# Storing the 0/1 matrices of layer 0 and loading them in layer 2, with two vector additions moved

## The chip, the cores and the metric

The kernel runs on 1 core of one Trainium2 chip, as one program. The metric is the device time of one execution, in microseconds (us). The engines are TensorE (PE in the profile, with its weight loads as PEld), VectorE (DVE), ScalarE (ACT), GpSimd (POOL) and SyncE (SP). They run side by side, each through its own instructions in order, and wait for one another through semaphores. The 16 DMA engines of the core are shared by the transfers that SP, ACT and POOL issue.

## The reference

The network has 50,000 nodes with 64 features and 25,000 edges, sorted by target node, and four residual layers. Cut to what matters:

```python
h = relu(layernorm(x));  x = x + L0(h)   # message passing: relu([h[src],h[dst]] @ W + b), mean by target, update
h = relu(layernorm(x));  x = x + L1(h)   # graph convolution: weighted sum by target, then @ W.T + b
h = relu(layernorm(x));  x = x + L2(h)   # attention over the edges of a target, Wo, FiLM, layer norm,
                                         # gelu MLP, then layer norm with ln2_g and ln2_b
h = relu(layernorm(x));  x = x + L3(h)   # exp(-t L) h as a Taylor series: powers of a sparse matrix B on h
```

Each layer gathers node rows for the edges and sums edge rows into nodes. Layers 0, 1 and 2 sum by target node, layer 3 by source node.

## The kernel before

The nodes are cut into NQ = 49 groups of 1,024 (8 blocks of 128). The edges of a group fill 5 tiles of 128 slots (TL = 245 tiles in all). A tile can only hold edges of a few blocks (the tables `BT` and `TB`), and for these pairs of tile and block the kernel makes 0/1 matrices on DVE by comparing numbers.

- `node_hot` (L1881) makes `s.noh`, nodes x slots: 8 comparisons a group, against the row of keys that `load_keys` (L1876) reads for all partitions. TensorE uses it to bring rows of node tables to the edges' slots (`to_slots`, and the loop of `logits` in layer 2).
- `slot_hot` (L1889) makes `s.soh`, slots x nodes: 5 comparisons a group. TensorE uses it to sum edges into nodes (`to_sums`, `to_nodes`).

Layers 0 and 2 make both matrices from the same keys; layer 1 makes `soh` alone; layer 3 has another order of edges and its own `soh`.

Each layer is a software pipeline over the 49 groups. `pipeline` (or `Steps` in layer 2) runs one stage of each group in flight, oldest group first, and a new group enters at each step. Layer 0 has the stages fetch, hots, message, sums, update, project; layer 1 has fetch, scaled, sums, turn, product. Layer 2 has an "up" pipeline (fetch, hots, logits) and a "down" pipeline (fetch2, message, sums, attend, turn, close, product, finish) with a `softmax` between them for each of 4 batches of 12 or 13 groups: while batch k goes up, batch k-1 goes down. So the first batch goes up alone and the last goes down alone. Layer 3 (fetch, scaled, sums) computes B h; then come the second power by pairs and the higher powers on short lists.

Rows of other nodes come by indirect DMA that POOL issues, 5 a group and layer (`gather`, L1006: `ga`, `gt`, `kvg`, `y`). POOL also issues the transfers of the lists for the higher powers (`nmap`, `lgot`, `lrow`). `build_lists` is cut into small pieces, and `lists_pace` lets some of them into the program after each stage (0.5 a stage in layer 0, 0.4 in layer 1, 1.2 in layer 2). A list of one level is found from the list of the level before, through DRAM: POOL scatters, SP loads (`lback`), DVE compares, POOL scatters and gathers again.

The order of each engine's instructions is laid down when the program is built, by a scheduler that starts from the order of the source and from its own estimate of times. Every instruction after that waits in its engine's line. Tiles live in pools with `bufs` buffers: a tile's next writer waits until the last reader is done. In layers 0 and 2 the pools have 2 buffers unless a tile says otherwise; the DMAs that SP and ACT issue take 8 semaphores in turn.

Other lines that matter: layer 1's `sums` adds (L2074) `x2` and stores it in `x2tab` from ACT (L2075); layer 2's `close` loads it again (L2357), and `finish` multiplies by ln2_g (L2378), adds ln2_b to x2 (L2379), adds both (L2380), takes the norm and relu to `h`, stores `h` in `h3tab` (L2383), adds `h` (L2384) and stores the sum in `xstab` (L2385). Layer 3's `sums` loads that sum and adds the first term of the series (L2502).

Of the kernel before, what the change touches and what calls it, by code (L numbers as in the profile page):

```python
# [59 lines left out]
GRP = ((0, 1), (1, 2), (3, 1), (4, 2), (6, 2))  # L60
OHW = (0, 384, 768, 1152, 1664, 1920)

POLY = np.ones(1)
# [903 lines left out]
def fast(ctx: ExitStack, tc: tile.TileContext, a: dict, out: bass.AP, flag: bass.AP):  # L967
# [913 lines left out]
    def node_hot(pool, s):  # L1881

        s.noh = pool.tile([P, 8, 2 * P], BF16, name="noh")
        for j in range(8):
            t0, n = BT[j]
            nc.vector.tensor_scalar(s.noh[:, j, :n * P], s.keys[:, t0 * P:(t0 + n) * P], pblk[:, j:j + 1], None,  # L1886
                                    op0=OP.is_equal)
# [10 lines left out]
    def to_slots(po, s, tab, start=True):  # L1898

        for i in range(5):  # L1900
            b0, nb = TB[i]
            for j in range(b0, b0 + nb):
                c = (i - BT[j][0]) * P
                for k in range(3):
                    nc.tensor.matmul(po[:, i, :], s.noh[:, j, c:c + P], tab[:, j, k * D:k * D + D],
                                     start=(start and j == b0 and k == 0), stop=(j == b0 + nb - 1 and k == 2))
# [68 lines left out]
    with tc.tile_pool(name="l0c", bufs=1) as cp, tc.tile_pool(name="l0", bufs=2) as pool, \  # L1975
# [67 lines left out]


    with tc.tile_pool(name="l1c", bufs=1) as cp, tc.tile_pool(name="l1", bufs=2) as pool, \
            tc.tile_pool(name="pl1", bufs=1, space=PSUM) as ps:
        b1l = bias_rows(cp, row_bcast("L1_gnn_b", pool=cp), "b1l")
        wkv = cp.tile([P, 4 * D], F32, name="wkv")
        cen = ident_less_mean(cp)
# [19 lines left out]
        def sums(q, s):  # L2069
# [34 lines left out]
    with tc.tile_pool(name="l2c", bufs=1) as cp, tc.tile_pool(name="l2", bufs=2) as pool, \  # L2104
# [105 lines left out]
        nc.vector.tensor_copy(zb[:, 1:2], pb)  # L2210
        g2n, b2n = row_bcast("L2_gnn_ln2_g", pool=cp), row_bcast("L2_gnn_ln2_b", pool=cp)

# [6 lines left out]
        def fetch(q, s):  # L2219
# [4 lines left out]
            nc.sync.dma_start(s.qt.rearrange("p b k d -> p b (k d)"), nodes(qtab, q))  # L2224
            load_keys(pool, q, s)
            s.typ = pool.tile([NE3, RW], F16, name="typ", bufs=2)
            nc.sync.dma_start(s.typ, ttab[q:q + 1, :].to_broadcast([NE3, RW]))

        def hots(q, s):
            s.types = pool.tile([NE3, RW], BF16, name="types")  # L2230
            nc.vector.tensor_scalar(s.types, s.typ, typei, None, op0=OP.is_equal)
            node_hot(pool, s)

        def logits(q, s):
# [18 lines left out]
            for i in range(5):  # L2253
                nc.tensor.matmul(pe[:, i, :], s.types[:, i * P:(i + 1) * P], etab[:, KW:], start=True, stop=False)
                b0, nb = TB[i]
                for j in range(b0, b0 + nb):
                    c = (i - BT[j][0]) * P
                    for k in range(3):
                        nc.tensor.matmul(pe[:, i, :], s.noh[:, j, c:c + P], s.qt[:, j, k, :], start=False,
                                         stop=(j == b0 + nb - 1 and k == 2))  # L2260
# [107 lines left out]
        def finish(q, s):  # L2368
# [9 lines left out]
            nc.vector.tensor_mul(x3, x3, along(g2n, 8))  # L2378
            nc.vector.tensor_add(s.x2, s.x2, along(b2n, 8))  # L2379
# [4 lines left out]
            nc.vector.tensor_add(x3, x3, h)  # L2384
            nc.scalar.dma_start(nodes(xstab, q), x3)  # L2385
# [95 lines left out]
    with tc.tile_pool(name="mps", bufs=1, space=PSUM) as mps, tc.tile_pool(name="l3", bufs=2) as pool, tc.tile_pool(name="pl3", bufs=2, space=PSUM) as ps:  # L2481
        def fetch(q, s):
# [177 lines left out]
```

## Time and profile before

| | us |
|---|---|
| median of 9 runs | 3656.36 (3638.07 to 3663.84) |
| the profiled execution, its own time | 3658.54 |
| its span | 3656.4 |
| lists and tables before layer 0 | 0 to about 650 |
| layer 0 | about 650 to 1390 |
| layer 1 | about 1390 to 1815 |
| layer 2 | about 1815 to 2860 |
| layer 3, B h | about 2860 to 3205 |
| second power, higher powers | about 3205 to 3656 |

The borders come from the starts of the lines that belong to each layer; neighbouring layers overlap a little. The profiled execution's time is 2.1 us over its span and 2.2 us over the median. In the views, "busy" is the union of an engine's instructions, "x" their number, and the time after the bar is how long the engine sat idle before them and what ended that.

### The profile page before, as it was taken

The page shows a single profiled execution, that of the slowest core. Times are in us where ns is not written, and L with a number is a line of the kernel's source. Part 1 is how long each engine was busy: PE and PEld are TensorE (multiplying, and loading weights), DVE is VectorE, ACT ScalarE, POOL GpSimd, SP SyncE. Part 2 cuts the span into 40 slices and gives each one's busy share as a digit, 9 for nine tenths or more (in the row PEclk, how much of TensorE's full clock was granted, in tenths as well). Part 3 has the DMA queues.
Part 4 walks back from the last instruction along what each step waited for, and adds up shares of the span by engine and source line. Part 5 has one row for each costly group of instructions (what it writes and reads, how often), then busy time and mean ns, then how long its engine had stood idle before and what let it go on. Part 6 is the DMA issues. An engine that isn't in the chain of part 4 may idle for free. (4 is left out here: it accounts for less than half of the span.)

```text
span 3656.4 us, 63671 instructions
## 1 busy us (share of the span) xinstructions
PE 2533.4 (69%) x21828; PEld 1787.6 (49%) x21828; DVE 2662.8 (73%) x8365; ACT 1325.7 (36%) x3056; POOL 2090.3 (57%) x1997
## 2 busy tenths in 40 slices
PE   7897774699999746777579766677677464466620
PEld 3324664577777634566455433344333354355520
DVE  9999998777778637999878766788888665455310
ACT  0002552222223314777504443445478333332000
POOL 0477777733333766666376775765100577775786
PEclk9755555755556766888758776778789675566555
DMA  1003772744445415877665333333222345488221
GB/s 53 6 4 111 210 231 85 199 123 114 118 120 144 125 32 156 239 234 237 182 197 150 103 102 96 99 114 108 67 91 77 113 126 153 148 232 229 44 25 11
DMA packets 528804, 457.79 MB, mean 125 GB/s; under 512 B 282147, under 2 KB 388802, under 8 KB 528340
## 3 DMA queue, kind: packets, MB, share of 16 engines
q1 hardware_dynamic: 361204, 263.52, 25.2%
q10 hardware_dynamic: 94032, 139.60, 11.0%
q0 software_dynamic: 73232, 50.49, 7.4%
q8 instruction: 174, 2.85, 0.3%
q14 instruction: 162, 1.33, 0.1%
HBM read 217.09 MB, written 237.38 MB: 124 GB/s over the span
## 5 line engine op out<-in xcount | busy, mean ns | idle before, releaser
L1006 POOL DMA_INDIRECT y<-h3tab,sptr x245 | 257.2, 1050 | 326.2 <-DVE soh L1894 251.8
L1006 POOL DMA_INDIRECT ga<-atab,nrs x245 | 246.8, 1007 | 327.2 <-DVE z L2003 157.8
L1006 POOL DMA_INDIRECT kvg<-kvtab,nrs x245 | 249.6, 1019 | 177.0 <-issue 64.6
L1006 POOL DMA_INDIRECT gt<-g1tab,nrs x245 | 253.1, 1033 | 149.9 <-issue 65.1
L1934 PEld LDWEIGHTS <-soh 128*128 128x128 bf16 x4410 | 224.2, 118 | 207.2 <-issue 193.5
L1924 PE MATMUL pa<-soh,m 128*64 128x256 bf16 (+1 forms) x2646 | 287.1, 334 | 38.0 <-ACT m L2006 27.3
L1006 POOL DMA_INDIRECT raw<-otab,nrd x196 | 195.0, 995 | 191.9 <-DVE bad L1152 132.5
L1011 POOL DMA_INDIRECT stab<-raw,pf x196 | 206.9, 1056 | 59.7 <-issue 59.7
L1924 PEld LDWEIGHTS <-m 128*64 128x64 bf16 x2646 | 179.6, 141 | 123.4 <-issue 52.8
L1006 POOL DMA_INDIRECT lgot<-nmap,ldst x183 | 184.6, 1009 | 60.8 <-issue 52.7
L1934 PE MATMUL po<-y,soh 128*128 128x64 bf16 x2205 | 123.9, 231 | 135.7 <-DVE y L1086 73.3
L1131 DVE TENSOR_REDUCE ln_v<-ln_sq 128x8 f32<-128x512 f32 x294 | 196.4, 679 | 24.9 <-ACT ln_sq L1144 18.9
L1894 DVE TENSOR_SCALAR soh<-it,key 128x384 bf16<-128x384 f16 (+2 forms) x735 | 206.2, 323 | 4.6 <-PE pa L1924 4.4
L1006 POOL DMA_INDIRECT y<-ftab,ldst x140 | 140.0, 1000 | 84.2 <-issue 74.0
L1144 ACT ACTIVATE ln_sq<-ln_xc 128x512 f32<-128x512 f32 x196 | 121.0, 626 | 175.5 <-DVE ln_xc L1142 164.1
L1886 DVE TENSOR_SCALAR noh<-keys,pblk 128x256 bf16<-128x256 f16 (+1 forms) x784 | 178.8, 290 | 3.9 <-DMA keys<-ktab 3.9
L1086 DVE TENSOR_TENSOR y<-y 128x320 f32<-128x320 f32 (+1 forms) x196 | 75.6, 390 | 144.1 <-ACT y L2493 120.7
L1189 PE MATMUL pab<-wab,tr 64*128 64x128 f32 x784 | 148.1, 431 | 32.6 <-ACT tr L1176 32.6
L1934 PE MATMUL po<-g,soh 128*128 128x64 bf16 x2205 | 121.0, 214 | 66.3 <-DVE g L1086 66.0
L1132 ACT ACTIVATE ln_v<-ln_v,epsc 128x8 f32<-128x8 f32 x294 | 83.4, 296 | 227.5 <-DVE ln_v L1131 205.4
L2352 PE MATMUL ph<-tr,w1z 128*128 128x512 f32 x196 | 144.4, 827 | 27.2 <-ACT tr L2346 27.0
L1189 PEld LDWEIGHTS pab<-wab,tr 64*128 64x128 f32 x784 | 134.1, 319 | 51.6 <-ACT tr L1176 51.3
(571 smaller groups left out, 7488.5 us busy)
## 6 DMA issues: line engine op xcount, KB each, us to landing
kvtab<-kv SPq DMA_DIRECT2D x49, 512.0 KB
xs<-xstab SPq DMA_DIRECT2D x98, 256.0 KB
ftab<-f ACTq DMA_DIRECT2D x98, 256.0 KB
xt<-in_x SPq DMA_DIRECT2D x96, 256.0 KB
btab<-bt ACTq DMA_DIRECT2D x49, 384.0 KB
bt<-btab SPq DMA_DIRECT2D x49, 384.0 KB
qtab<-qt ACTq DMA_DIRECT2D x49, 384.0 KB
qt<-qtab SPq DMA_DIRECT2D x49, 384.0 KB
```

Of the source, the lines that this page charges most:

```text
L1006: return nc.gpsimd.indirect_dma_start(out=dst, out_offset=None, in_=tab[:, :], in_offset=IndirectOffsetOnAxis(ap=idx, axis=0))
L1011: return nc.gpsimd.indirect_dma_start(out=tab[:, :], out_offset=IndirectOffsetOnAxis(ap=idx, axis=0), in_=src, in_offset=None, bounds_chec ...
L1086: nc.vector.tensor_sub(x3[:, :, k, :], x3[:, :, k - 1, :], h[:, :, k - 1, :])
L1131: nc.vector.tensor_reduce(v, sq, AX.X, OP.add)
L1132: nc.scalar.activation(v, v, AF.Sqrt, bias=epsc, scale=1.0 / D)
L1144: nc.scalar.activation(sq, xc, AF.Square)
L1189: nc.tensor.matmul(pab[:, i, :], s.tr[r, i, :], wab[r, :], start=True, stop=True)
L1886: nc.vector.tensor_scalar(s.noh[:, j, :n * P], s.keys[:, t0 * P:(t0 + n) * P], pblk[:, j:j + 1], None, op0=OP.is_equal)
L1894: nc.vector.tensor_scalar(oh[:, OHW[i]:OHW[i + 1]], it16[:, b0 * P:(b0 + n) * P], keys[:, q, i:i + 1], None, op0=OP.is_equal)
L1924: nc.tensor.matmul(o, l, r, start=first, stop=last)
L1934: nc.tensor.matmul(po[:, j, :], oh[:, c:c + P], msg[:, i, k, :], start=(not started and i == t0 and k == 0), stop=(end and (not started or ...
L2352: nc.tensor.matmul(ph, w1z[h], s.tr, start=True, stop=True)
```

## The change

Layer 0 stores both matrices of each group in a new DRAM table, `noh` from SP and `soh` from ACT (491,520 bytes each). Layer 2 no longer makes them: it loads `noh` in the stage fetch of the up pipeline, in place of the keys, and `soh` in fetch2 of the down pipeline, each with 3 buffers. `noh` is stored without gaps (`NOH`), 1,920 columns. Layer 1 adds ln2_b to x2 before it stores it, in a tile of its own, so that layer 2 need not. Layer 2 stores its x without `h`; layer 3 loads `h` beside it and adds it in its stage scaled.

```diff
+NOH = (0, 128, 384, 640, 896, 1152, 1408, 1664)
+    ohtab = dram.tile([NQ * P, 2, OHW[-1]], BF16, name="ohtab")
...
     def node_hot(pool, s):
-        s.noh = pool.tile([P, 8, 2 * P], BF16, name="noh")
+        s.noh = pool.tile([P, OHW[-1]], BF16, name="noh")
...
         def message(q, s):                       # layer 0
+            nc.sync.dma_start(ohtab[P * q:P * q + P, 0, :], s.noh)
+            nc.scalar.dma_start(ohtab[P * q:P * q + P, 1, :], s.soh)
             pe = ps.tile([P, 5, D], F32, name="pe", bufs=2)
...
             nc.vector.tensor_add(x2, s.x1, po)   # layer 1, sums
-            nc.scalar.dma_start(nodes(x2tab, q), x2)
+            x2b = pool.tile([P, 8, D], F32, name="x2b")
+            nc.vector.tensor_add(x2b, x2, along(b2n, 8))
+            nc.scalar.dma_start(nodes(x2tab, q), x2b)
...
-            load_keys(pool, q, s)                # layer 2, fetch
+            s.noh = pool.tile([P, OHW[-1]], BF16, name="noh", bufs=3)
+            nc.sync.dma_start(s.noh, ohtab[P * q:P * q + P, 0, :])
...
-            node_hot(pool, s)                    # layer 2, hots
...
+            s.soh = pool.tile([P, OHW[-1]], BF16, name="soh", bufs=3)   # layer 2, fetch2
+            nc.sync.dma_start(s.soh, ohtab[P * q:P * q + P, 1, :])
...
-            s.soh = slot_hot(pool, key, q)       # layer 2, message
...
-            nc.vector.tensor_add(s.x2, s.x2, along(b2n, 8))   # layer 2, finish
             nc.vector.tensor_add(x3, x3, s.x2)
...
             nc.scalar.dma_start(nodes(h3tab, q), h)
-            nc.vector.tensor_add(x3, x3, h)
             nc.scalar.dma_start(nodes(xstab, q), x3)
...
+            s.h = pool.tile([P, 8, D], F32, name="h", bufs=3)   # layer 3, fetch
+            nc.sync.dma_start(s.h, nodes(h3tab, q))
...
             s.soh = slot_hot(pool, skey.rearrange("p (q i) -> p q i", i=5), q)   # layer 3, scaled
+            nc.vector.tensor_add(s.xs, s.xs, s.h)
```

More of the change, by code (lines that the diff above doesn't have):

```diff
@@ L1881, in node_hot @@
     def node_hot(pool, s):
-        s.noh = pool.tile([P, 8, 2 * P], BF16, name="noh")
+        s.noh = pool.tile([P, OHW[-1]], BF16, name="noh")
         for j in range(8):
             t0, n = BT[j]
-            nc.vector.tensor_scalar(s.noh[:, j, :n * P], s.keys[:, t0 * P:(t0 + n) * P], pblk[:, j:j + 1], None,
+            nc.vector.tensor_scalar(s.noh[:, NOH[j]:NOH[j] + n * P], s.keys[:, t0 * P:(t0 + n) * P], pblk[:, j:j + 1], None,
                                     op0=OP.is_equal)
@@ L1902, in to_slots @@
             for j in range(b0, b0 + nb):
-                c = (i - BT[j][0]) * P
+                c = NOH[j] + (i - BT[j][0]) * P
                 for k in range(3):
-                    nc.tensor.matmul(po[:, i, :], s.noh[:, j, c:c + P], tab[:, j, k * D:k * D + D],
+                    nc.tensor.matmul(po[:, i, :], s.noh[:, c:c + P], tab[:, j, k * D:k * D + D],
                                      start=(start and j == b0 and k == 0), stop=(j == b0 + nb - 1 and k == 2))
@@ L2047, in fast @@
         b1l = bias_rows(cp, row_bcast("L1_gnn_b", pool=cp), "b1l")
+        b2n = row_bcast("L2_gnn_ln2_b", pool=cp)
         wkv = cp.tile([P, 4 * D], F32, name="wkv")
@@ L2210, in fast @@
         nc.vector.tensor_copy(zb[:, 1:2], pb)
[L2211 removed]
+        g2n = row_bcast("L2_gnn_ln2_g", pool=cp)
         batches = [(0, 13), (13, 12), (25, 12), (37, 12)]
@@ L2256, in logits @@
                 for j in range(b0, b0 + nb):
-                    c = (i - BT[j][0]) * P
+                    c = NOH[j] + (i - BT[j][0]) * P
                     for k in range(3):
-                        nc.tensor.matmul(pe[:, i, :], s.noh[:, j, c:c + P], s.qt[:, j, k, :], start=False,
+                        nc.tensor.matmul(pe[:, i, :], s.noh[:, c:c + P], s.qt[:, j, k, :], start=False,
                                          stop=(j == b0 + nb - 1 and k == 2))
```

## The prediction

> **What bounds the kernel now.** I read first the busy time of each engine by stage, because the whole-span shares (DVE 73%, PE 69%) average over stages with different limits. The columns are the stretch, its length, busy us of PE, PEld, DVE, ACT and POOL with the number of instructions, the granted TensorE clock, the share of the DMA engines and GB/s.
>
> ```profile
> core 0: us, PE busy (x) PEld busy (x) DVE busy (x) ACT busy (x) POOL busy (x), PEclk, DMA share, GB/s
> 650.00:735.00 85.00, 60.58 (x802) 49.08 (x802) 65.36 (x236) 26.73 (x71) 62.41 (x64) 0.82 0.89 227
> 735.00:1170.00 435.00, 420.71 (x3696) 336.38 (x3692) 335.04 (x1220) 113.42 (x291) 147.45 (x144) 0.57 0.44 120
> 1170.00:1390.00 220.00, 138.03 (x1414) 110.79 (x1413) 124.34 (x409) 51.72 (x130) 138.47 (x145) 0.69 0.31 88
> 1420.00:1780.00 360.00, 275.41 (x3239) 218.65 (x3237) 331.12 (x943) 265.61 (x814) 226.81 (x220) 0.85 0.78 234
> 1815.00:1910.00 95.00, 66.53 (x745) 49.82 (x745) 69.10 (x293) 8.62 (x35) 69.86 (x72) 0.50 0.69 201
> 1910.00:2070.00 160.00, 134.03 (x1197) 81.18 (x1197) 132.80 (x396) 76.66 (x134) 115.66 (x112) 0.82 0.44 131
> 2070.00:2360.00 290.00, 186.49 (x1314) 110.49 (x1313) 201.20 (x641) 115.48 (x196) 205.20 (x197) 0.71 0.32 95
> 2360.00:2610.00 250.00, 188.76 (x1398) 110.33 (x1397) 212.09 (x730) 122.92 (x208) 123.72 (x114) 0.78 0.34 106
> 2610.00:2860.00 250.00, 168.83 (x822) 84.88 (x820) 206.48 (x430) 171.15 (x251) 0.00 (x0) 0.81 0.23 79
> 2890.00:3200.00 310.00, 163.71 (x2245) 143.16 (x2246) 177.12 (x447) 108.68 (x309) 235.25 (x224) 0.63 0.47 142
> ```
>
> The limits differ. Layer 0 (rows 1 to 3): DMA near its limit for the first 85 us (0.89), then PE (421 of 435 us), then POOL. Layer 1 (row 4): DVE, 331 of 360 us. Layer 2 is rows 5 to 9, cut at the softmaxes; I call them A to E. B h (row 10): POOL. POOL's waits show an "issue" of 0.3 us before nearly every indirect DMA, so POOL is full at busy + 0.31 x count: A 92 of 95 us, B 150 of 160, C 266 of 290, D 159 of 250, E 0, and B h 305 of 310. So in A to C, POOL's gathers and lists set the pace whatever DVE does; only D and E can be DVE's.
>
> Then what POOL waited for in D (us in total, times, longest):
>
> ```profile
> POOL nmap L1011 <- DVE lval L1639: 28.7, 2, 20.7
> POOL lrow L1011 <- DVE ldest L1545: 25.4, 2, 19.6
> POOL kvg L1006 <- DVE lnrow L1635: 18.1, 1, 18.1
> POOL nmap L1011 <- DVE vv L2249: 13.2, 1, 13.2
> POOL lrow L1011 <- DVE vv L2249: 6.1, 1, 6.1
> ```
>
> All 91 us of them end with DVE: here the lists wait in DVE's line. Last, the groups that the change touches (busy us, mean ns, idle before):
>
> ```profile
> L1894 DVE TENSOR_SCALAR soh<-it,key 128x384 bf16<-128x384 f16 (+2 forms) x735 | 206.2, 323 | 4.6 <-PE pa L1924 4.4
> L1886 DVE TENSOR_SCALAR noh<-keys,pblk 128x256 bf16<-128x256 f16 (+1 forms) x784 | 178.8, 290 | 3.9 <-DMA keys<-ktab 3.9
> L2384 DVE TENSOR_TENSOR x<-x,h 128x512 f32<-128x512 f32 x49 | 33.7, 687 | 0.0
> L2379 DVE TENSOR_TENSOR x<-x,b_L_gnn_ln_b 128x512 f32<-128x512 f32 x49 | 33.4, 681 | 5.6 <-DMA x<-x2tab 5.6
> ```
>
> **What leaves DVE in layer 2.** Neighbouring comparisons overlap, so I take busy time, not mean: `noh` 178.8/784 = 0.228 us, x 392 = 89.4; `soh` 206.2/735 = 0.281, x 245 = 68.7; the two adds 33.4 and 33.7. Sum 225 us: per group 1.82 on the way up and 2.77 on the way down, 4.59 for a step of both.
>
> - A: POOL is full; 0. B: of 160 us, 10 are POOL waiting for DVE; I take 3. C: POOL idles 24 us, once 25.4 us long for `vv`, but DVE itself stood then 25.1 us for `lback`, a list's transfer. A faster DVE comes to that wait earlier and gains nothing. I take 6.
> - D: 12 steps x 4.59 = 55 us of DVE's 212. If only the 91 us of list waits shrink in that ratio (26%), 24 us; if DVE alone sets the pace, 55. PE, busy 189 of 250, would have little slack at 195, so I take 35.
> - E: from 2640 to 2820 us a group takes 13.1 us (by the starts of L2384); there DVE is busy 150 of 180 us, PE 142, ACT 138: 10.9, 10.3 and 10.1 us a group. Without 2.77, DVE falls to 8.2 and PE is next. In the built order ACT has 43 table loads after the last softmax instead of 58 (1.283 us each), 1.6 us a group less, so ACT is not. PE's matmul tiles `pa` and `po` have one buffer each, used twice a group, so PE will not run gapless: 10.6 us a group. 12 x 2.5 = 30, and 4 for the drain, whose chain loses one add: 34.
>
> Layer 2: 3 + 6 + 35 + 34 = **78 us less**. Ends: 34 (E alone) and 180 (DVE sets the pace everywhere, 225 x 0.8, DVE's busy share).
>
> **What comes to layer 1.** One add a group, 128x512 f32, by the row of L2379 0.69 us: 49 x 0.69 = 33.6 us on an engine that is 92% busy. Between nothing (hidden in the 8% idle) and 33.6 I take **28 us more**. The store of `x2tab` on ACT now waits for this add; the Square queued behind it waits for a later DVE instruction anyway, so that costs 0 (0.69 a group at most, inside the same 33.6). The broadcast of ln2_b moves to layer 1's constants: one small load, nothing in either place.
>
> **What comes to layer 0.** 49 stores of `noh` on SP, 49 of `soh` on ACT, 983 KB a group. Layer 1's row (234 GB/s at share 0.78) makes 300 GB/s of a full DMA, so 3.3 us a group. In the first 85 us a group takes 9.2 us at 0.89, that is 8.2 us of DMA; 11.5 with the stores, 2.3 more for six groups, 14 us. From 735 to 1170 a group takes about 15 us, 6.7 of it DMA: 10 of 15, hidden behind PE. After 1170 POOL hides it. On ACT a DMA issue like `x1tab`'s takes 0.33 us and ACT is busy 113 of 435 us; behind it wait the relu and `cat` copies. `noh` and `soh` have two buffers, and now are free only when the store has landed. I take **15 us more**. Ends: 0, and 45 if the slow early groups let TensorE's clock fall sooner (0.82 in the first row, 0.57 in the second, where a group takes 6 us longer: 5 groups x 6 = 30).
>
> "DMA: Bandwidth & Descriptors" of the Trainium skill ("Issuing engines are not separate DMA queues") says that transfers issued from SP and ACT end on the same DMA engines, so splitting the two stores buys only issue time. That speaks against hiding them where the row shows 0.89, and would leave the 14 us as they stand.
>
> **SP's queue and the loads in layer 2.** `noh` takes the place of the keys' load in fetch, 328 KB a group more, and `soh` joins fetch2 with 491 KB; at 300 GB/s 1.1 and 1.6 us of DMA. In A, where only `noh` comes, a step of 7 us holds 0.69 x 7 = 4.8 us and then 5.9; elsewhere 2.7 us come to steps of 13 to 24 us at 0.44 or less. I take 0; if A's steps were full, it would cost 13 x 1.1 = 14. Behind the `soh` load on SP stand the loads of `h2`, `x2` and `lback`; three buffers release it when `sums` of three groups before is done, so it is early. In layer 1 nothing is loaded anew.
>
> **What comes to B h.** 49 adds `xs + h` (33.6 us of DVE, busy 177 of 310) and 49 loads of 256 KB, at DMA share 0.47. POOL is full there, so only what slows POOL counts. From 2970 to 3050 us, where DVE is crowded, POOL's gathers start every 1.404 us (median) instead of 1.249: 0.155 x 49 = 8. The add stands before `y`'s split and waits for two loads, but four and three buffers fetch ahead. I take **5 us more**, ends 0 and 12.
>
> "SBUF — State Buffer" of the Trainium skill ("Who interferes with whom") says that a DVE instruction with two SBUF inputs holds up a GpSimd instruction that reads SBUF until it is through. By that, each add could cost a gather up to 0.69 us, 34 us in the stage instead of 5; the trace does not show stalls of that size behind the ordinary adds of layer 1, where gathers last 1.03 us in the mean.
>
> **The sum.** -78 + 28 + 15 + 5 = -30. The profiled execution took 3658.5 us (span 3656.4 plus 2.1), so 3628.5; it lies 2.2 over the median of the runs shown: **3626 us**. From the terms' ends without the rivals' extremes, this case runs from -75 to +8. About 0.3%, 11 us, is what a measurement of this kernel can tell from no change.
>
> **Rivals.**
> 1. *Layer 0's stores gate its buffers (slower).* SP already stands 155 us in all for TensorE before loads of `bt` (L1988, 22 times); a `noh` store behind such a load leaves late, the comparisons of two groups later wait for its landing, and PE for them. Full price 49 x 3.3 = 161 us, giving -78 + 28 + 5 + 161 = +116, 3772 us. Slower begins where layer 0 grows by 45 + 11 = 56 us, 1.15 a group. For it: the 0.89. Against: the 0.44 with 15 us steps, in which a store has time.
> 2. *The lists, not DVE, pace D.* Each level needs scatter, load, compare, scatter, gather; if the transfers set D, only E's 34 us come: -34 + 48 = +14, 3670 us. For it: the 25 us on `lback` in C; against: D's waits all end with DVE.
> 3. *DVE paces all of layer 2.* -180 + 28 + 15 + 0 = -137, 3519 us. Against: POOL full in A to C.
>
> **How the numbers follow.** Forecast 0.61 (0.46 faster, 0.12 same, 0.03 slower); rival 1 0.15, slower; rival 2 0.16 (0.02, 0.03, 0.11); rival 3 0.08, faster. That makes 0.56 faster, 0.15 same, 0.29 slower. The likeliest case's own range is 3581 to 3664. Both signs hold much, so the range reaches into rivals 1 and 2 and leaves out their far end and rival 3: 3570 to 3685.
>
> **What would show it.** Right: A, B, C within 10 us of 95, 160, 290; E near 10.6 us a group with PE its busiest engine; layer 1 at 8.6 us a group; D about 215 us; layer 0 longer only before 735 us. Wrong: layer 0's steps of 15 us longer with PE waiting for `noh`; D unchanged with POOL waiting for list transfers; POOL idle in A to C; DVE waiting for `noh` or `soh` loads.

## The result and the profile after

The changed kernel is slower: 3703.26 us median of 14 runs (3683.96 to 3721.32) against 3652.54 of 46 runs before, a ratio of 1.0139, interval 1.0122 to 1.0156. Some 51 us were lost where 26 to 30 were to be gained. The profiled execution took 3696.24 us, its span is 3694.5.

First the same view as before, busy time by engine and stage. Layer 2's rows are cut at the softmaxes of this trace: B is 1910 to 2084, then C, D, and E to 2885.

```profile
core 0: us, PE busy (x) PEld busy (x) DVE busy (x) ACT busy (x) POOL busy (x), PEclk, DMA share, GB/s
735.00:1170.00 435.00, 417.56 (x3795) 333.08 (x3795) 342.37 (x1253) 115.46 (x295) 151.13 (x147) 0.60 0.65 196
...
1420.00:1780.00 360.00, 265.10 (x3043) 213.93 (x3044) 337.59 (x826) 263.47 (x799) 235.75 (x213) 0.83 0.79 231
1910.00:2084.00 174.00, 127.86 (x1187) 81.44 (x1187) 114.22 (x374) 68.99 (x124) 111.78 (x111) 0.76 0.56 179
2084.00:2374.00 290.00, 161.90 (x1351) 98.11 (x1352) 156.11 (x467) 110.38 (x195) 195.10 (x193) 0.74 0.42 133
2374.00:2629.00 255.00, 174.25 (x1367) 103.11 (x1365) 165.92 (x553) 112.39 (x202) 118.95 (x117) 0.78 0.44 140
2629.00:2885.00 256.00, 173.05 (x865) 90.89 (x864) 173.08 (x335) 152.81 (x240) 8.13 (x4) 0.79 0.32 102
2913.00:3235.00 322.00, 160.12 (x2236) 138.80 (x2237) 199.38 (x491) 107.65 (x310) 248.27 (x224) 0.64 0.57 169
```

DVE did become freer in B to E: 133, 201, 212, 206 us before, 114, 156, 166, 173 now. No stage became shorter for it. Layer 0 carries the stores (196 GB/s instead of 120) at the same length. Where did DVE's free time go? Its waits for the lists' transfers between 1806 and 2640 us (us in total, times, longest), first before, then after:

```profile
DVE lsrc L1566 <- DMA lback<-lrow: 26.7, 3, 25.1
DVE lpi L1612 <- DMA kvg<-kvtab,nrs: 20.3, 2, 15.2
...
DVE lpi L1612 <- DMA lgot<-nmap,ldst: 11.3, 1, 11.3
...
DVE kk L2248 <- DMA kvg<-kvtab,nrs: 5.6, 3, 3.8
```

```profile
DVE lpi L1614 <- DMA kvg<-kvtab,nrs: 65.8, 2, 37.8
DVE lsrc L1568 <- DMA lback<-lrow: 51.3, 5, 26.9
DVE kk L2256 <- DMA kvg<-kvtab,nrs: 50.7, 10, 18.7
...
DVE lpi L1614 <- DMA lgot<-nmap,ldst: 33.5, 3, 18.3
...
DVE lraw L1552 <- DMA lrow<-lraw,ldest: 8.6, 1, 8.6
```

`lpi`, `lsrc` and `lraw` are the steps with which a list takes over what POOL scattered, SP loaded or POOL gathered. DVE stood 159 us before them, 58 before the change (where `kvg` is named as the last, I take it for a gather that POOL issued among the list's own). The `kk` row is the groups' own wait for their gathers, which POOL issues in one line with the lists' transfers: 51 us, 6 before. By stage, the lists' waits were 52 us in C and 7 in D before (5.1 for `lpi`, 1.7 for `lsrc`), and 101 and 58 after. D's part after the change is the 33.5 us for `lpi` above and

```profile
DVE lsrc L1568 <- DMA lback<-lrow: 24.4, 4, 13.0
```

The table sums up the spans. "A to D" runs from the last gather of layer 1 to the last softmax, E from there to the first gather of `h3tab`, B h to the last one; "left" is how many of the 49 groups had not begun their attend at the last softmax. The borders are rounded to 1 us, so a span can be off by 1.

| us | layer 1 | A to D | E | left | A to E | B h |
|---|---|---|---|---|---|---|
| before | 418 | 854 | 250 | 15 | 1104 | 331 |
| after | 423 | 875 | 256 | 16 | 1131 | 344 |

Layer 0's last gather ends at 1340 us before and 1331 after. So of the 38 us of span that were lost, layer 0 gave 9 back, and layer 1 took 5, A to D 21 (A 7, B 9, C and D 2 to 3 each), E 6, B h 13 and what follows 2.

### The profile page after: what moved, and what is told of

Read it like the earlier page. It is cut to its first block, busy times and chain, and to the rows that moved or that the text cites. A ratio compares the mean times of both kernels' runs of the same rounds, so it can differ in the third digit from the quotient of the medians.

```text
span 3694.5 us, 63376 instructions
## 1 busy us (share of the span) xinstructions
PE 2475.7 (67%) x21828; PEld 1765.3 (48%) x21828; DVE 2536.0 (69%) x7728; ACT 1284.3 (35%) x3025; POOL 2100.5 (57%) x1997
## 5 line engine op out<-in xcount | busy, mean ns | idle before, releaser
L1008 POOL DMA_INDIRECT y<-h3tab,sptr x245 | 269.6, 1100 | 318.1 <-DVE soh L1896 243.8
L1008 POOL DMA_INDIRECT kvg<-kvtab,nrs x245 | 241.3, 985 | 214.6 <-issue 66.1
L1008 POOL DMA_INDIRECT gt<-g1tab,nrs x245 | 268.4, 1095 | 138.8 <-issue 61.7
L1936 PEld LDWEIGHTS <-soh 128*128 128x128 bf16 x4410 | 215.2, 116 | 253.5 <-issue 236.8
L1926 PE MATMUL pa<-soh,m 128*64 128x256 bf16 (+1 forms) x2646 | 272.5, 318 | 65.7 <-ACT m L2010 56.4
L1926 PEld LDWEIGHTS <-m 128*64 128x64 bf16 x2646 | 165.5, 133 | 133.1 <-ACT m L2010 60.2
L2603 POOL DMA_INDIRECT out<-y,lnode x85 | 132.3, 1556 | 38.2 <-issue 26.5
L1896 DVE TENSOR_SCALAR soh<-it,key 128x384 bf16<-128x384 f16 (+2 forms) x490 | 142.7, 325 | 2.6 <-PE pa L1926 2.4
L2361 PE MATMUL ph<-tr,w1z 128*128 128x512 f32 x196 | 128.9, 745 | 22.9 <-ACT tr L2355 22.3
```

The source lines that it names most:

```text
L1008: return nc.gpsimd.indirect_dma_start(out=dst, out_offset=None, in_=tab[:, :], in_offset=IndirectOffsetOnAxis(ap=idx, axis=0))
L1896: nc.vector.tensor_scalar(oh[:, OHW[i]:OHW[i + 1]], it16[:, b0 * P:(b0 + n) * P], keys[:, q, i:i + 1], None, op0=OP.is_equal)
L1926: nc.tensor.matmul(o, l, r, start=first, stop=last)
L1936: nc.tensor.matmul(po[:, j, :], oh[:, c:c + P], msg[:, i, k, :], start=(not started and i == t0 and k == 0), stop=(end and (not started or ...
L2361: nc.tensor.matmul(ph, w1z[h], s.tr, start=True, stop=True)
L2603: st = nc.gpsimd.indirect_dma_start(out=out[:, :], out_offset=IndirectOffsetOnAxis(ap=s.node[:, t:t + 1], axis=0), in_=sums[k][:, t, :], i ...
```

## The experiments

**1. The parts of the change.** Three kernels make a part of it alone: the matrices stored and loaded (both additions stay where they were), the two additions moved (no matrix stored or loaded), and layer 0's stores alone (nothing loads them). A fourth is the changed kernel with two buffers for `po` in layer 2 and one for `pv`. What each adds to the kernel before (the first three) or to the changed one:

```diff
+            nc.sync.dma_start(ohtab[P * q:P * q + P, 0, :], s.noh)      # first and third: the stores
+            nc.scalar.dma_start(ohtab[P * q:P * q + P, 1, :], s.soh)
...
+            nc.sync.dma_start(s.noh, ohtab[P * q:P * q + P, 0, :])      # first: the loads
+            nc.sync.dma_start(s.soh, ohtab[P * q:P * q + P, 1, :])
...
+            nc.vector.tensor_add(x2b, x2, along(b2n, 8))                # second: the additions
+            nc.vector.tensor_add(s.xs, s.xs, s.h)
...
-                pv = ps.tile([P, 3, KW], F32, name="pv", bufs=2)        # fourth
+                pv = ps.tile([P, 3, KW], F32, name="pv", bufs=1)
-            po = ps.tile([P, 4, 2, D], F32, name="po")
+            po = ps.tile([P, 4, 2, D], F32, name="po", bufs=2)
```

> The 0/1 matrices are stored in layer 0 and loaded in layer 2, and both additions stay where they were before. Theory P (layer 2 is paced by POOL with its lists in stages A to D and by the one buffer of the PSUM tile po in E, so that relief of DVE gains nothing): layer 2 lasts as long as before within 20 us, E stays at about 13 us a group, B h stays at about 331 us, and the time is 5 to 30 us over before. Theory T (the relief of DVE is real, and the 101 MB more of transfers take it away): nearly all of the loss is here, 40 to 50 us over before, and DVE waits for loads of noh or soh.

> Both additions are moved (ln2_b to layer 1, x + h to B h) and nothing is stored or loaded of the 0/1 matrices. Theory P: the 67 us of DVE that leave layer 2 bring nothing there, layer 1 hides its addition (it did in the changed kernel), B h is 10 to 15 us longer because POOL's gathers last 1.10 us instead of 1.05: 8 to 20 us over before. Theory T: without the transfers of the matrices DVE's relief shows: 0 to 30 us under before.

> Layer 0 stores both matrices, layer 2 makes its own as before and loads nothing of them; the additions stay where they were. Theory P: within 6 us of before, since TensorE paces layer 0 and the stores lie beside it. Theory T: 10 to 25 us over before, in layer 0.

> The changed kernel with two buffers for the PSUM tile po of layer 2 and one for pv instead of two (the banks are full). Theory P: in E a group falls from 13 us to 11 or less, which takes 25 to 35 us from the changed kernel's 3703; the up-only stage A may lose a few us by the single pv. Theory T: E stays at 13 us a group, and the time at that of the changed kernel within 6 us.

Measured, against 3645.59 for the kernel before on the same chip:

| | median us | ratio, interval | A to D | E | B h |
|---|---|---|---|---|---|
| matrices alone | 3711.45 | 1.0184 (1.0145 to 1.0223) | 896 | 252 | 332 |
| additions alone | 3731.20 | 1.0226 (1.0186 to 1.0266) | 906 | 259 | 344 |
| stores alone | 3660.96 | 1.0039 (1.0016 to 1.0062) | 855 | 248 | 336 |
| `po` doubled | 3699.07 | 1.0158 (1.0117 to 1.0198) | 873 | 253 | 345 |

Each half alone costs more than both together (for the matrices alone the interval still touches that of the whole change, 1.0122 to 1.0156), so the account by parts does not add up: something that depends on the whole is at work. For both halves theory P had expected far less, 5 to 30 us and 8 to 20, so it missed as well. Theory T falls with the second, since the additions alone, with no transfer of a matrix, cost the most. The stores are nearly free: 15 us in the median, none of it in layer 0 by the trace (last gather at 1335 us). One `po` buffer does not hold E: that part of theory P falls. And B h is the one place with a plain price: 332 without the added `x + h`, 344 with it (331 to 336 in the kernel before and the runs without it of parts 1 and 2, 340 to 345 in those with it). The groups of its gathers, in the changed kernel and in the one with the matrices alone (busy, mean ns):

```profile
L1008 POOL DMA_INDIRECT y<-h3tab,sptr x245 | 269.6, 1100 | 318.1 <-DVE soh L1896 243.8
```

```profile
L1008 POOL DMA_INDIRECT y<-h3tab,sptr x245 | 257.3, 1050 | 314.4 <-DVE soh L1896 240.0
```

12.3 us of POOL over 49 groups, each with an addition and a load more, is 0.25 us a group, on an engine that is full: the whole of the 12 us. In layer 1, where the change adds an addition and no load, the gathers of `g1tab` went the same way: 1033 ns in the mean before and 1095 after, 253.1 and 268.4 us for 245. Without the layer 1 addition they took 1028 and 1030 ns (matrices alone, stores alone), with it and no transfer of a matrix 1099. So an addition on DVE is enough to make the gathers longer.

The additions alone show something else. The 0.69 us a group that layer 1's DVE took on lengthened layer 1 by 5 us at most; they pushed the lists' own instructions out of it. In the trace of before, DVE has 62.9 us of list instructions (durations added up; neighbours overlap) in 1420 to 1800 us and 81.8 in 1806 to 2640; after, 22.8 and 122.1; with the additions alone, 121.8 in the second stretch, with the matrices alone 77.4. In the built order the 77 comparisons of the level-3 list (`ljunk`) stand ahead of the first up step of layer 2 in the kernel before, and behind up steps 13 to 21 in the changed one. With the matrices alone they stand where they stood before, and there another thing moved: 26 of the list's scatters stand among A's gathers on POOL, where the kernel before has none, and A takes 173 us instead of 149. So the lists' place moved in both halves, in different ways.

**2. Is it POOL?** In both kernels layer 2's gathers were replaced by one plain load a group, which leaves out the choice of the rows:

```diff
-            for i in range(5):
-                gather(s.kv[:, i, :], kvtab, nrs[:, q, i:i + 1])
+            nc.sync.dma_start(s.kv ..., kvtab ... [:, 1024 * q:1024 * q + 640])
```

> The kernel before, in which layer 2's 245 gathers of kvtab (five a group, on POOL) are replaced by one contiguous load a group of as many bytes from SP; it leaves out the choice of the rows. POOL keeps only the lists' own scatters and gathers in layer 2. Theory Q (the up steps of stages A to D are paced by POOL and by the place that the lists' pieces take in the queues): with POOL free, A to D are next bound by DVE, which was busy 69, 133, 201 and 212 us of the 95, 160, 290 and 250 us of A, B, C and D: the four stages give back 60 to 100 of their 795 us, stage E stays near 250, the run takes 3545 to 3590. Rival V (DVE already paces B and D of the kernel before): under 25 us back, the run over 3620.

> The changed kernel with the same replacement of the 245 gathers of kvtab by contiguous loads (leaves out the choice of the rows). Theory Q: with POOL out of the way, the DVE time taken from layer 2 shows: in this trace DVE was busy 55, 114, 156 and 166 us of A to D, about 124 less than before, so this kernel is the faster one of the pair by 20 to 60 us: A to D give back 100 to 170 us against the changed kernel with its gathers, the run takes 3510 to 3575. Rival V (something else that the change brings, its transfers or its loads, holds layer 2 up): this kernel stays slower than or level with the kernel before under the same replacement.

3590.17 us, ratio 0.9828 (0.9805 to 0.9851), and 3641.63, ratio 0.9968 (0.9947 to 0.9989). A to D give back 52 us in one and 54 in the other (802 and 821 are left): POOL's gathers cost both the same, and the changed kernel stays the slower by 51 us. Theory Q falls as the cause of the difference, since it had the changed kernel ahead; there rival V holds. For the kernel before V missed (under 25 us back) and Q came near (60 to 100 us of A to D). With the gathers gone the two traces part clearly. In B the changed kernel is the shorter, 118 us against 162, with fewer of the lists' transfers there (41 against 75); in A (170 against 151) and C that is lost again. Stage C, the kernel before, then the changed one, then what the latter's DVE waited for most in it:

```profile
2051.00:2291.00 240.00, 181.07 (x1308) 106.82 (x1309) 198.19 (x630) 113.65 (x193) 122.34 (x112) 0.74 0.39 113
```

```profile
2054.00:2346.00 292.00, 172.63 (x1361) 104.68 (x1360) 158.31 (x471) 110.79 (x197) 142.13 (x139) 0.71 0.43 134
```

```profile
DVE lpi L1614 <- DMA lgot<-nmap,ldst: 68.4, 2, 41.1
```

The kernel before works (198 of 240 us); the changed one does less and takes longer, once 41 us standing before one `lpi` while POOL makes that list's 42 gathers, one every 1.25 us. The kernel before waits 4.2 us for list transfers in all of A to D.

**3. What is E?** The changed kernel with a square for the Gelu of layer 2, which leaves the Gelu out:

```diff
-            nc.scalar.activation(s.hid[:, h, :], ph, AF.Gelu, bias=b1m)
+            nc.scalar.activation(s.hid[:, h, :], ph, AF.Square, bias=b1m)
```

> The changed kernel with a square in the place of layer 2's Gelu (it leaves the Gelu out), so that ACT need not change its tables twice a group for it: in stage E of the changed kernel 45 table loads took 57.7 us of ACT, 1.28 us each. Theory L (stage E is a loop of latencies through engines none of which is full: normalisation, transposes, the two hidden halves, the next group's attend): every load on the loop is saved, at least the one before the square root, so E goes from 256 to 205 to 235 us and the run to 3655 to 3685. Rival F (E is held by PE's order or the loads of noh and soh): E stays within 6 us of 256, since ACT was busy only 153 of 256 us.

3609.87 us, ratio 0.9878 (0.9848 to 0.9907). E takes 193 us instead of 256, more than expected; rival F falls. The activation itself is no faster (684 ns in the mean, 686 with the Gelu). ACT's table loads in E of the changed kernel (two groups of them) come to 45 of 1.283 us; one is left without the Gelu. The kernel before, shown first, has 59:

```profile
L1132 ACT ACT_TABLE_LOAD x30 | 38.5, 1283 | 5.4 <-DVE x L2384 5.0
L2353 ACT ACT_TABLE_LOAD x29 | 37.2, 1283 | 0.5
```

```profile
L1134 ACT ACT_TABLE_LOAD x23 | 29.5, 1283 | 0.4
L2362 ACT ACT_TABLE_LOAD x22 | 28.2, 1283 | 12.7 <-DVE x L2388 12.4
```

```profile
2620.00:2813.00 193.00, 139.07 (x819) 73.19 (x819) 168.11 (x331) 92.47 (x193) 3.25 (x3) 0.90 0.42 132
```

A group of E takes 13.0 us before, 13.7 after and 9.7 here (means of the last 12 steps between attends): 4.0 us less, where the loads took 57.7 of 256 us, 3.1 us a group, though ACT was busy only 153 of the 256 us. So E is a loop of waits (attend, normalisation, transposes, hidden, attend of the next group), no engine in it is full, and the 33 us that DVE is less busy there after the change were taken beside the loop. How much of the loop is table loads is less clear: the changed kernel has 14 of them fewer in E than the kernel before, 18 us, and its E is no shorter. The square's run also had one group fewer left (15) and a higher granted clock in E, 0.90 against 0.79; what each is worth was not separated. Without the loads DVE is at 168 of 193 us: only then would the change have something to relieve there, which no run tried.

**4. Are the lists in the way?** In both kernels the lists' pace in layer 2 was set to 0, so that they come behind the groups. A further run raised the pace in layer 1:

```diff
-        lists_pace.rate = 0.4       # layer 1, one run of the changed kernel
+        lists_pace.rate = 0.8
...
-        lists_pace.rate = 1.2       # layer 2, both kernels
+        lists_pace.rate = 0
```

> The changed kernel with the lists' pace in layer 1 raised from 0.4 to 0.8 items a stage: in the built order of DVE the 77 compares of the level-3 list's link now stand ahead of the first up step of layer 2, as in the kernel before, and not behind up steps 13 to 21. Theory Q: the late link cost stage B about 10 us and POOL's idle time 51 us; with the link ahead, and the level-3 list's 42 scatters of its map moved into layer 1 where POOL has room (236 of 360 us busy), A to D return to 790 us or less from 815, and may fall to 740 (42 x 1.25 us less POOL work); layer 1, whose DVE is busy 338 of 360 us, pays up to 24 us for the link. The run takes 3650 to 3695. Rival (the place of the lists has no part in it): A to D stay at 815 and the run at 3700 to 3725.

> The changed kernel with the lists given out after layer 2's groups (pace 1.2 to 0 in layer 2), again, on a chip where the kernel before takes some 3650 us. Theory W (in the changed kernel the lists' transfers hold DVE in layer 2): from the last gather of layer 1 to stage E it took 875 us in the changed kernel and 854 in the kernel before; this run takes 675 to 755, at least 40 less than the kernel before under the same edit. Rival G (the groups' own steps, gathers or loads set the pace): 800 to 875, and no shorter than the kernel before under the same edit. Stage E and what follows get longer by the lists' work in either theory, 250 to 350 us of POOL in all, of which E can take some 200. The run: 3600 to 3760.

> The kernel before with the same edit. Theory W: DVE is near full here without the lists' waits (its own work in A to D is some 615 us, 82 us of it for the lists), so from the last gather of layer 1 to stage E it takes 770 to 830 against 854. Rival G: as long as, or shorter than, the changed kernel under the same edit. The run: 3600 to 3740.

More pace in layer 1: 3753.69 us, ratio 1.0264 (1.0204 to 1.0324), a clear miss. The comparisons stood ahead of the up steps as meant, but from layer 1's last gather to the first softmax it took 237 us instead of 157: 62 of the list's scatters and gathers now stood among A's gathers in POOL's queue, and 62 x 1.25 is 78. In A, POOL has no room.

No pace in layer 2: 3690.95 us, ratio 1.0101 (1.0069 to 1.0132), for the changed kernel and 3826.81, ratio 1.0476 (1.0435 to 1.0518), for the kernel before. In this pair the changed kernel is the faster one, by 136 us. B, C, D and E of the changed kernel, then B, C and D of the kernel before:

```profile
1911.00:2031.00 120.00, 109.40 (x1111) 71.65 (x1110) 90.80 (x229) 59.88 (x109) 64.65 (x65) 0.82 0.79 259
2031.00:2177.00 146.00, 128.76 (x1164) 79.56 (x1162) 117.53 (x298) 79.73 (x149) 62.32 (x60) 0.82 0.68 218
2177.00:2326.00 149.00, 130.15 (x1229) 80.16 (x1227) 128.12 (x325) 88.28 (x166) 46.35 (x45) 0.90 0.64 208
2326.00:2841.00 515.00, 252.34 (x1251) 134.57 (x1251) 268.70 (x784) 206.85 (x328) 231.46 (x232) 0.71 0.25 76
```

```profile
1898.00:2058.00 160.00, 131.78 (x1201) 80.32 (x1200) 134.84 (x396) 78.74 (x137) 66.97 (x67) 0.82 0.48 136
2058.00:2286.00 228.00, 181.28 (x1322) 106.78 (x1322) 184.51 (x503) 112.75 (x196) 63.26 (x61) 0.78 0.41 122
2286.00:2515.00 229.00, 180.11 (x1307) 106.89 (x1308) 182.51 (x489) 112.78 (x194) 45.69 (x44) 0.78 0.36 107
```

A to D take 572 us in the changed kernel and 766 in the other, 194 less, which tells theory W from rival G. Not all of it is gain. At the last softmax the changed kernel had 22 groups left and the other 16: its up steps had run ahead of its down steps. At 13.7 us, a group's step in E of the changed kernel, those 6 groups are by estimate 82 us that went from A to D into E. From A to E the pair takes 1087 and 1173 us, 86 apart, and the rest of the 136 lies behind, where the kernel before has more of the lists still to do (67 of their scatters and gathers stand behind E, 22 in the changed kernel). So without the lists the change is worth about 86 us in layer 2; with the lists there it is worth nothing. But the lists' time comes back: E is 515 us (407 in the kernel before, whose DVE waits alike), with these waits in the changed kernel's E:

```profile
DVE lpi L1614 <- DMA lgot<-nmap,ldst: 107.7, 3, 59.0
DVE lraw L1552 <- DMA lrow<-lraw,ldest: 48.5, 5, 15.7
```

In the changed kernel A to E fell from 1131 to 1087 us, and the stages behind paid 43 for the rest of the lists (9 in B h, 34 up to the end). In the kernel before A to E rose from 1104 to 1173.

The pair had first been run on another chip, together with a pair in which the lists pause longer:

```diff
-                self.credit = -2 * self.rate
+                self.credit = -10 * self.rate     # in layer 2
```

> The changed kernel with the lists' pace in layer 2 set from 1.2 to 0: their items are given out after layer 2's groups, so that stages A to D hold no gather or scatter of the lists, and the stages behind do. Theory W (what the relieved DVE does in layer 2 of the changed kernel is wait for the lists' own transfers: between 1806 and 2640 us it waited 159 us for lgot, lback, lrow and the kvg transfers queued with them, against 58 us before, because its order holds the lists' next step ahead of up steps that could run): A to D fall from 817 us by 120 to 200, to at most 700, and are at least 20 us shorter than those of the kernel before under the same edit. Rival G (the groups' own steps, their gathers or their loads pace A to D): they fall by under 70. The run's time is open, since the lists' work then lengthens the stages behind: 3640 to 3800.

> The kernel before with the same edit. Theory W: here DVE itself was nearly full once the gathers were gone (29 of 30 us in most slices of the run without gathers), and waited only 58 us for the lists, so A to D fall from 795 us to between 680 and 740, by less than in the changed kernel: the DVE time of the 0/1 matrices now shows as the difference of the pair. Rival G: both fall alike, and the changed kernel's A to D stay the longer ones by some 20 us. The run's time is open for the same reason: 3620 to 3780.

> The changed kernel in which, in layer 2, the lists pause for ten items' credit and not two wherever their next step needs the transfers of the one before: in the built order the level-4 list's first step then stands behind 20 ended groups and not 13, so the transfers have more time, and the lists end in stage E. Theory W: DVE waits for the lists under 110 us between 1806 and 2640 us, against 159, and A to D fall by 30 to 80 us, the run to 3625 to 3680. Rival G: A to D stay within 15 us of 817.

> The kernel before with the same longer pauses. Theory W: it waited only 58 us for the lists, so it has less to gain: A to D fall by 0 to 35 us, the run takes 3615 to 3660, and the pair's difference shrinks from 51 us to under 30. Rival G: nothing moves, and the pair's difference stays.

On that chip the kernel before took 4943.06 us, and layer 0 began at some 1096 us instead of 654 to 660, so these times stand beside no other run here. In order they were 4832.24, 4900.30, 4847.32 and 4917.52 us, all below the kernel before there (ratios 0.9773, 0.9912, 0.9798, 0.9933), while the same pair without pace lay 1.0% and 4.8% above it on the chip of the rows above. The changed kernel as it is was not run on that chip, so what it would be worth there is not known. A to D without the lists took 719 us in the changed kernel and 852 in the other: the same sign, again with 22 and 16 groups left. With longer pauses they took 1024 and 1112 us; what that would be elsewhere is open.

**5. Can the loss be got back?** Two pairs. In the first the lists' pace in layer 2 is 0.5 instead of 1.2, in both kernels, and in the changed one `x + h` goes back to layer 2. In the second the steps that receive a list's transfer keep the place of the source on DVE (the scheduler may not pull them forward), the pauses are longer, and again `x + h` goes back:

```diff
-        nc.vector.tensor_scalar(lev[:, :c], got[:, :c], 16, None, op0=OP.arith_shift_right)
+        tc.keep_in_program_order(nc.vector.tensor_scalar(lev[:, :c], got[:, :c], 16, None, op0=OP.arith_shift_right))
...
-        lists_pace.rate = 1.2
+        lists_pace.rate, lists_pace.gap = 1.2, 10      # the pause, 2 before; in stage E: 2.0, 3
```

> The changed kernel with two edits: x + h stays in layer 2 (a load and an add a group less in the stage of B h), and the lists' pace in layer 2 is 0.5 and not 1.2, so that they spread over A to E instead of ending ahead of E. Theory W: A to D fall by 60 to 130 us against the changed kernel, stage E takes the rest of the lists in POOL's and DVE's free time (POOL idle, DVE 173 of 256 us) and grows by 10 to 60, the stage of B h returns from 344 to about 332; the run takes 3560 to 3650 and beats both kernels. Rival G: only the 13 us of B h come back, 3680 to 3700.

> The kernel before with the lists' pace in layer 2 at 0.5. Theory W: less to gain, since DVE waited 58 us for the lists and not 159, and its own work fills it: 3610 to 3655, at least 20 us slower than the changed kernel with the same pace and x + h in layer 2. Rival G: within 15 us of 3650.

> The changed kernel with x + h back in layer 2, and the steps of the lists that receive a transfer (lpi, lsrc, the clearing of lraw) kept in program order on DVE with a pause of ten items' credit ahead of them (three, at a pace of 2.0, in stage E), so that the groups' steps stand ahead of them: in the built order the level-3 list's lpi comes behind 33 up steps and not 27, the last lists' behind 48 of 49 attends. Theory W: DVE's waits for the lists' transfers from 1800 us to the stage of B h fall from some 170 us to under 80, layer 2 (last gather of layer 1 to the stage of B h) takes 1020 to 1085 us against 1131 in the changed kernel and 1104 before, the run 3585 to 3650: it beats both kernels. Rival H (the lists are a chain of POOL's transfers whose length layer 2 has to hold, wherever its waits stand): layer 2 takes 1090 to 1131 us, the run 3655 to 3700.

> The kernel before with the same two edits to the lists. Theory W: its DVE waited 58 us for the lists, so it gains 0 to 30 us, 3620 to 3660, and is 10 to 60 us slower than the changed kernel treated alike. Rival H: within 15 us of 3650, and level with the changed kernel treated alike or faster.

| | median us | ratio, interval | A to D | E | left | A to E | B h |
|---|---|---|---|---|---|---|---|
| changed, pace 0.5 | 3703.75 | 1.0125 (1.0062 to 1.0188) | 710 | 424 | 20 | 1134 | 320 |
| before, pace 0.5 | 3732.84 | 1.0203 (1.0152 to 1.0254) | 785 | 335 | 15 | 1120 | 357 |
| changed, in order | 3676.18 | 1.0095 (1.0060 to 1.0130) | 729 | 375 | 22 | 1104 | 332 |
| before, in order | 3629.18 | 0.9955 (0.9929 to 0.9981) | 809 | 283 | 16 | 1092 | 329 |

The pace of 0.5 moved time from A to D into E and gained nothing; both expectations of theory W missed, but for the order of the pair (the changed kernel 29 us ahead, where 20 were expected). Keeping the order did what it was meant to do to the waits: from 1800 to 2870 us DVE of the changed kernel waited for one kind of list transfer alone,

```profile
DVE lsrc L1568 <- DMA lback<-lrow: 20.2, 2, 15.0
```

and A to D fell by 146 us. Other waits came in their place. In the same stretch DVE stood 114 us for the groups' own gathers (`kk`; 51 in the changed kernel), and POOL, which issues them behind the lists' transfers, stood 97 us for `lraw`, a step of the lists that DVE now reaches later. And the run stayed slower than the kernel before, as rival H expected (A to E 1104, within its 1090 to 1131; the run 3676.18, within its 3655 to 3700). E took 375 us, 119 more:

```profile
2498.00:2873.00 375.00, 243.48 (x1225) 129.88 (x1226) 269.90 (x702) 209.26 (x327) 90.93 (x88) 0.79 0.30 99
```

The column "left" tells the larger part. The up steps had run ahead of the down steps: at the last softmax 22 groups had still to attend, not 16, and a group took 13.7 us in E of the changed kernel: by estimate 6 x 13.7 = 82 of the 119. The rest fits the lists' steps that now lie in E (a group takes 15 us there), but was not separated. The kernel before, treated alike, had 16 groups left (15 as it was), its list waits from 1806 to 2640 us fell from 58 to 3.3 us, and of the versions that compute everything, run where the kernel before takes some 3650 us, it is the one that beats both kernels, by 0.45%.

## Why the prediction was wrong

The forecast was 3626 us, 77 too low, and the range ended at 3685. By its own steps:

- **D, 35 us less; measured 3 to 5 more.** This is the step that failed first. The working read "all 91 us of them end with DVE: here the lists wait in DVE's line" and let those waits shrink with DVE's work. The wait goes both ways: a list's next step also stands in DVE's queue until POOL's transfers for the last one have landed, and everything behind it stands too. In D DVE was busy 46 us less (212 to 166), and its waits for list transfers grew by 51 (7 to 58): what was taken from its work came back as waiting. For C the working had said just that of `lback` ("a faster DVE comes to that wait earlier and gains nothing") and had not carried it to D, nor to a loss. That the lists in the queues take the gain away is shown by the pair without lists: 1087 us against 1173 from A to E, and 136 us in the whole run, for the changed kernel. That DVE's waits are the way in which they do it is argued, not shown: over the runs the waits and the time do not go together (58 us of waits and 854 us of A to D before, 72 and 906 with the additions alone, 144 and 896 with the matrices alone, 159 and 875 after), and with the waits nearly gone in part 5 A to E was only 27 us shorter. Rival H, that layer 2 has to hold the lists' chain of transfers however the waits fall, would fit both.
- **E, 34 us less; measured 6 more.** As large an error as D's. "PE is next", at 10.6 us a group, took the busiest engine's share as the bound; a group took 13.7. (It also counted 12 groups for E, where 15 had still to attend.) E is a loop through all engines; of the two to three table loads of 1.283 us a group, on an engine that was 60% busy, some are on it, and DVE's 2.77 us were not. The reading of ACT ("ACT is not") was right as to its load and wrong as to its part. Its count of fewer loads came true (45 for 59) and gained nothing. "ScalarE: Activation LUTs" of the Trainium skill ("What ACT_TABLE_LOAD costs") counts a drain of 1.38 us beside the 1.283 of every load, 2.66 in all; by that the 45 loads would, by estimate, be 120 us of E. The run without 44 of them gave 63 us in all, 1.4 a load, with the one group fewer and the higher clock inside it.
- **A to C, 9 us less, for POOL being full.** Right that the change gains nothing there as it stands; C went from 288 us to 290, A from 149 to 157 and B from 164 to 173, where the list comparisons that layer 1 gave up now stand. But POOL being full was not the whole reason: with the groups' gathers gone from POOL the changed kernel's C was no shorter (292 us, POOL busy for 142). And "whatever DVE does" holds only with the lists there: without them B and C took 120 and 146 us in the changed kernel and 160 and 228 in the other.
- **Layer 1, 28 us more; measured 5.** The engine was full, but what gave way was not the layer: 40 us of list instructions left it for layer 2. What they cost there was not measured by itself.
- **Layer 0, 15 us more; measured none** (its last gather 9 us earlier). The row for 735 to 1170 us has the stores in the DMA share, 0.44 to 0.65, and PE as full as before. The Trainium skill's rule that SP's and ACT's transfers end on the same DMA engines ("DMA: Bandwidth & Descriptors", "Issuing engines are not separate DMA queues") agrees with the share, but the 14 us did not come: from 650 to 735 us the row went from 227 to 286 GB/s and the share to 0.94, so 0.89 had not been full. Rival 1 falls with it.
- **B h, 5 us more, ends 0 and 12; measured 13 (12.3 unrounded).** Mechanism right, size off: 0.25 us a group on POOL, where 0.1 was taken. The Trainium skill's rule that a DVE instruction with two SBUF inputs holds up GpSimd instructions that read SBUF ("SBUF — State Buffer", "Who interferes with whom") points the same way, though the section adds that `tensor_tensor` had not been seen to stall DMAs; its full hold, up to 34 us, did not come. Layer 1's gathers, longer by 0.06 us each with an addition and no load added, speak for the addition and not for the 49 loads; that it acts through the port, no run here shows.
- **The rivals.** Rival 2 named the cause, that the lists' transfers and not DVE set the pace, at 0.16. Its 3670 us was too low since it kept E's 34 us and let the lists be neutral; they were a loss. Of the signs of being wrong, an unchanged D came, but POOL's longest waits there (28.1, 17.5 and 15.2 us) still ended with DVE, as before; it was DVE that stood for list transfers and for `kvg`. For the loads of `noh` or `soh` no engine that computes waited before the last softmax.

The sum by the runs: A to E 27 us more where 78 less were forecast, an error of 105; layers 0 and 1 together 4 less where 43 more were forecast, 47 back; B h 8 more than forecast, the rest 2. That is 68, and the profiled execution, forecast at 3628.5, took 3696.24. The remaining 9 to the medians' 77 are where the two profiled executions lie beside their medians (2 above the runs then shown, 7 below).

What stays open: the price of the displaced list work, that of the longer list waits and that of the lists' chain itself could not be put apart (each half of the change costs A to D 42 to 52 us, both together 21); why E did not shorten with 14 table loads fewer; and whether some order lets the changed kernel keep what it gains without the lists. Three tries did not find it.

## What to carry to other kernels

Idle time of a queue has two ends: before counting on a relieved engine, list what it waits for itself in that stage, and reckon that those waits may grow by what is taken from the work ahead of them (here 51 us for 46 in D). Where a side task is threaded through an engine's queue by counting steps, a change to the steps changes where the side task stands and how long it stands there: retune its place together with the change, and test a stage with the side task taken out of both versions, since that shows what the steps alone are worth. Compare the two where the same work has been done: a stage can look shorter because a part of the groups went on to the next one. And where no engine is near full, as in E (DVE 206 of 250 us at most), look for a loop: count what lies on the loop, a table load of an idle engine too, and not the busiest engine.

## What the runs showed of the hardware

A gather by POOL, or a scatter of the lists, took 0.96 to 1.11 us in the mean of its kind, with 0.3 us between two: at 1.25 us from one to the next, 42 of them are over 50 us, three to four groups' steps, and the receiving step was reached 41 us too early. An addition of 128x512 f32 a group on DVE made the gathers longer, by 0.06 us each in layer 1, where no load was added, and by 0.05 in B h. Removing 3.1 us of ACT table loads a group shortened E's loop by 4.0 us a group, with the granted clock at 0.90 there instead of 0.79; what the other 0.9 us were was not separated. Between the two kernels 14 such loads fewer in E shortened nothing. And DMA at a share of 0.89 still took another 59 GB/s, at 0.94, and layer 0 was not longer for it.
